# Moving GpSimd's sums of x1T ahead of other sums, and dealing the steps anew, in a graph kernel on one core

## The chip, the core and the metric

The kernel runs on one core of a Trainium2 chip. The metric is the device time of one execution in microseconds (us); of several runs the median is given.

## What is computed

The reference takes a batch of 64 graphs with 256 nodes and 512 features, x (64, 256, 512), a dense weighted adjacency adj (64, 256, 256), a node mask, and weights of 512 x 512, all float32:

```python
h = relu(adj @ (x @ W1) + b1)
h = relu(adj @ (h @ W2) + b2)
x1 = layernorm(x + adj @ (h @ W3) + b3)
q, k, v = x1 @ Wq, x1 @ Wk, x1 @ Wv
agg = adj @ (k * mask)
w = mask * sum(q * agg, axis=-1) / sqrt(512)
out = layernorm(x1 + softmax(w over the nodes) * v)
```

The layer norms have no weights. The kernel uses that q * agg summed over features is the row-wise product of x1 @ M with adj @ (mask x1), where M is the product of Wq and the transpose of Wk. So Wk is never applied to a batch.

## The kernel before

**Tiling.** Two graphs are a pair, so there are 32 pairs. A pair goes through three stages, each written as a Python generator that issues a few instructions at every step:

- `front` (F): the three layers of the first network. Per layer, `support` (L225) multiplies activations by W, and `aggregate` (L244) multiplies by adj and applies relu. The third layer ends with its support. 29 steps.
- `back` (B): adj times the third support (the steps "t"), plus x and b3; the first layer norm, which gives x1; adj @ (mask x1), called `gather` in the code (the steps "g"); and per graph the **double product** x1 @ [Wv | M] (`attention`, L422, the steps "A"), with the score w.
- `finish` (E): softmax of w over the nodes, its product with v, the sum with x1, the second layer norm, the output.

In round i, F works on pair i, B on pair i - 1 and E on pair i - 2. The strings `ORDER`, `START` and `END` (L507 to L509) say in which order the three are advanced, one letter for one step. `START` is for the first round, where B is `make_m` (L174), which computes M; `END` is for the last, where F is done. The instructions are thus laid out by hand[...].

**Seven products instead of eight.** Supports, adj products and the double product all go through `seven` (L96). It splits both operands into 2 x 2 blocks and computes the product with seven block products, P1 to P7, in the order P1, P7, P6, P2, P5, P3, P4, one per step. The price is sums: of the stationary operand, four tiles S (`a_sums`, L203, or `adj_sums` for adj), and of the moving one, four tiles T (`b_sums`, L84). P1, P6, P5 and P3 accumulate in one PSUM bank. After P1, P6 and P5 ScalarE copies the bank out (L103, L112, L120), and the next of them may write only then. P7 and P4 share a second bank; after P5, VectorE reads it for the fourth block, and P4 may write only then. In `seven` the only own product between P6 and P5 is P2, and between P5 and P3 there is none, so what stands there comes from the other stages.

A product of a support or of the double product is a *long* step on TensorE, one of an adj product (L285) a *short* one. An aggregate has four long steps, named by their output column blocks: c2, c3, c0, c1.

**Sums.** `a_sums` returns three functions: `first` issues S[2] (L211, needed by P7), `rest` issues S[0] and S[1] (L214 and L215, needed by P5 and P6), `last` issues S[3] (L218, needed by P3). For the activations hT, `first` is issued after c3, `rest` after c1, `last` inside the next support. For x1T, the transposed x1, all three are issued after the gather (L468 to L470), in a step of their own without a product. In the text they are S2, S0, S1 and S3. All of them run on GpSimd, the last round's sums of x1T excepted. GpSimd also makes the T sums of the adj products (L87 to L90), adds x to copies (L65), adds b3 to x (L65), and sums adj (L65).

**x1T.** Except in the last round, VectorE transposes 32 x 32 blocks of x1 (L407), SP writes them to DRAM (L410, "via") and reads them back as x1T in four transfers (L412). In the last round TensorE transposes (L398).

**Loads.** SP's queue issues all DMAs: xT, the four blocks of W1, adj, the biases, W2, W3, the second adj, b3 and the mask, in this order. A W block comes as 128 x 2 x 256, 256 KB. VectorE makes the T sums of W1, W2 and W3 as soon as they arrive, then `mask_s` (L166), and only then the first sums of the supports. adj of pair i + 2 is loaded right after the gather (L467).

**Buffers.** [...] There are 11 S tiles, 4 T tiles, 7 support tiles, one x1T and two adj tiles.

Of the kernel before, what the change touches and what calls it, by code (L numbers as in the profile page):

```python
# [9 lines left out]
FP = mybir.dt.float32  # L10
# [4 lines left out]
P = 128  # L15
PAIR = 2
G = PAIR
# [3 lines left out]
def gcn_then_graph_attention(ctx: ExitStack, tc: tile.TileContext, xT, xN, adjT, mask, W1, b1, W2, b2, W3, b3,  # L21
# [15 lines left out]
    nc = tc.nc  # L37
    NPAIR = xT.shape[0]
    N, D = 256, 512
    NH, DC = N // P, D // P  # L40
    HD = D // 2
# [4 lines left out]
    const = ctx.enter_context(tc.tile_pool(name="const", bufs=1))  # L46
# [5 lines left out]
    E = mybir.EngineType  # L52
    ctx.enter_context(tc.manual_schedule(engines={E.PE, E.DVE, E.Activation, E.Pool, E.SP}))

    def bank(shape=(P, G, N)):
        return psum.tile(list(shape), FP, name="ps", tag="ps")

    def tmp():
        return pool.tile([P, D], FP, name="tmp", bufs=6)
# [5 lines left out]
        nc.gpsimd.tensor_tensor(o, a, b, op=op)  # L65


    def load_xT(i):
        t = pool.tile([P, DC, G, N], FP, name="xT", bufs=1)
        nc.sync.dma_start(t, xT[i].rearrange("p (c g n) -> p c g n", c=DC, g=G))  # L70
        return [t[:, :2], t[:, 2:]]

    def load_adj(i):
        t = pool.tile([P, NH, G, N], FP, name="aT", bufs=2)
        nc.sync.dma_start(t, adjT[i].rearrange("p (k g n) -> p k g n", k=NH, g=G))
        return t
# [7 lines left out]
    def b_sums(B, Ts, eng):  # L84

        sub = OP.subtract
        eng.tensor_tensor(Ts[2], B[3], B[1], op=sub)  # L87
        eng.tensor_tensor(Ts[0], B[1], B[0], op=sub)  # L88
        eng.tensor_tensor(Ts[1], B[3], Ts[0], op=sub)  # L89
        eng.tensor_tensor(Ts[3], B[2], Ts[1], op=sub)  # L90
# [43 lines left out]
    def load_w(w, n):  # L134


        q = []
        for k in (1, 0):
            for j in range(2):
                if (k, j) == (1, 1):  # L140
                    t = tmp().rearrange("p (c f) -> p c f", c=2)
                else:
                    t = const.tile([P, 2, HD], FP, name=f"w{n}_{k}{j}")
                q.append(t)
                nc.sync.dma_start(t, w[k * HD:(k + 1) * HD, j * HD:(j + 1) * HD].rearrange("(c p) f -> p c f", p=P))
        ts = [const.tile([P, 2, HD], FP, name=f"w{n}_{s}") for s in KEYS]
        b_sums(q, ts, nc.vector)
        return {1: q[0], 2: q[2], 3: q[3], 4: ts[3], 5: ts[0], 6: ts[1], 7: ts[2]}

    xTs = load_xT(0)  # L150
    wl = [load_w(W1, 1)]
    aTs = {0: load_adj(0)}
    bcol = []
    for n, b in ((1, b1), (2, b2)):
        t = const.tile([P, DC], FP, name=f"b{n}")
        nc.sync.dma_start(t, b)
        bcol.append(t)
    wl.append(load_w(W2, 2))
    wl.append(load_w(W3, 3))
    aTs[1] = load_adj(1)  # L160
    b3b = const.tile([P, D], FP, name="b3b")
    nc.sync.dma_start(b3b, b3.partition_broadcast(P))
# [1 line left out]
    nc.sync.dma_start(mask_t, mask.rearrange("p (h b) -> p h b", h=NH))  # L164
    mask_s = const.tile([P, NH, NPAIR * G], FP, name="mask_s")
    nc.vector.tensor_scalar(mask_s, mask_t, ISCALE, None, op0=OP.mult)  # L166
    ident = const.tile([P, P], FP, name="ident")
    make_identity(nc, ident)
    eps = const.tile([P, 1], FP, name="eps")
    nc.vector.memset(eps, EPS)  # L170

# [2 lines left out]
    def make_m():  # L174

        wq = pool.tile([P, DC, D], FP, name="wqT", tag="r", bufs=1)
        qk = [[wq[:, d] for d in range(DC)],
              [pool.tile([P, D], FP, name="wkT", tag="T", bufs=4) for _ in range(DC)]]
        for d in range(DC):
            for t, w in ((qk[0][d], WqT), (qk[1][d], WkT)):  # L180
                nc.sync.dma_start(t, w[d * P:(d + 1) * P, :])
        m = [pool.tile([P, 2, D], FP, name="m0", tag="v", bufs=2), const.tile([P, 2, D], FP, name="m1")]
        v0 = const.tile([P, 2, D], FP, name="v0")
        nc.sync.dma_start(v0, Wv[:HD].rearrange("(c p) f -> p c f", p=P))
        v1 = const.tile([P, 2, D], FP, name="v1")
        nc.sync.dma_start(v1, Wv[HD:].rearrange("(c p) f -> p c f", p=P))
        yield
        for f in range(DC):
            pt = bank((P, D))
            for d in range(DC):  # L190
                for j in range(DC):
                    nc.tensor.matmul(pt[:, j * P:(j + 1) * P], lhsT=qk[0][d][:, f * P:(f + 1) * P],  # L192
                                     rhs=qk[1][d][:, j * P:(j + 1) * P], start=(d == 0 and j == 0),
                                     stop=(d == DC - 1), skip_group_check=True)
            nc.scalar.copy(m[f // 2][:, f % 2, :], pt)
            yield
        ts = [const.tile([P, 2, D], FP, name=f"mv_{s}") for s in KEYS]
        b_sums((v0, m[0], v1, m[1]), ts, nc.gpsimd)
        mv.update({1: v0, 2: v1, 3: m[1], 4: ts[3], 5: ts[0], 6: ts[1], 7: ts[2]})
        yield  # L200

# [72 lines left out]
    def t_sums(B):  # L274
        Ts = [pool.tile([P, G, HD], FP, name="T", tag="T", bufs=4) for _ in range(4)]
        b_sums((B[0][0], B[0][1], B[1][0], B[1][1]), Ts, nc.gpsimd)
        return Ts
# [76 lines left out]
    def back(i, C, aS, x, end):  # L354
# [20 lines left out]
        b = i * G  # L375
# [11 lines left out]
        hg = [(h, g) for h in range(NH) for g in range(G)]  # L387
        xmb = [[xm[:, :, h, j * HD:(j + 1) * HD] for j in range(2)] for h in range(2)]
        if end:
            x1T = pool.tile([P, 2, 2, G, N], FP, name="x1T", bufs=1)  # L390
            x1b = lambda h, k: x1T[:, k, :, :, h * P:(h + 1) * P]
            for h, g in hg:
                apply(h, g)
            Ts = t_sums(xmb)
            for h, g in hg:
                pt = bank((P, 2, 2, P))
                for c in range(DC):
                    nc.tensor.transpose(pt[:, c // 2, c % 2], r[:, g, h, c * P:(c + 1) * P], ident)  # L398
                (nc.scalar.copy if h else nc.vector.tensor_copy)(x1T[:, :, :, g, h * P:(h + 1) * P], pt)
        else:  # L400
            tr = pool.tile([P, 4, 32, NH, 2, 2, G], FP, name="tr", tag="gt", bufs=1)
            x1T = pool.tile([P, P, NH, 2, 2, G], FP, name="x1T", bufs=1)
            x1b = lambda h, k: x1T[:, :, h, k].rearrange("p n c g -> p c g n")
            for h, g in hg:
                apply(h, g)
                for k in range(2):
                    nc.vector.transpose(tr[:, :, :, h, k, :, g].rearrange("p q j c -> p c q j"),  # L407
                                        r[:, g, h, k * HD:(k + 1) * HD].rearrange("p (c q j) -> p c q j", c=2, q=4))
            via = dram.tile([4, P, D], FP, name="via")
            nc.sync.dma_start(via.rearrange("q p e -> p q e"), tr.rearrange("p q j h k c g -> p q (j h k c g)"))  # L410
            for q in range(4):
                nc.sync.dma_start(x1T[q * 32:(q + 1) * 32].rearrange("p (a j) h k c g -> p a (j h k c g)", a=4),  # L412
                                  via[q].rearrange("(a i) e -> i a e", a=4))
            yield
            Ts = t_sums(xmb)
# [3 lines left out]
        w = small.tile([P, NH, G], FP, name="w", bufs=2)  # L419
        vs = [None] * G  # L420

        def attention(g):  # L422
# [12 lines left out]
            def c22(ps, t):  # L435
# [5 lines left out]
        gather = adj_times(aS, xmb, Ts, lambda y, t: add(gb(0, 0), y, t), lambda x: nc.scalar.copy(gb(0, 1), x),  # L441
                           lambda v, t: add(gb(1, 0), v, t), lambda v, t: add(gb(1, 1), v, t))
        src, first, rest, last = a_sums(x1b, nc.vector if end else nc.gpsimd)
        if end:
            first()
            rest()
            last()
            one = attention(0)
            for k in "GMGMGMGMGGGMMM":
                next(gather if k == "G" else one)  # L450
                yield
            for _ in gather:
                pass
            for _ in one:
                pass
            tail = finish(i, (r, vs, w), [0])
            for _ in attention(1):
                next(tail, None)
                yield
            for _ in tail:  # L460
                pass
            for _ in finish(i, (r, vs, w), [1]):
                pass
            return
        yield from gather
        if i + 2 < NPAIR:
            aTs[i + 2] = load_adj(i + 2)  # L467
        first()  # L468
        rest()
        last()  # L470
        yield
        for g in range(G):
            yield from attention(g)
        return r, vs, w
# [29 lines left out]
            nc.sync.dma_start(out[i, :, g * NH * D:(g + 1) * NH * D].rearrange("p (h f) -> p h f", h=NH), vs[g])  # L504


    ORDER = ("F E F" + " B F" + " B F E" * 5 + " B F B F F B B F F B F" + " B F"*3 + " B F E"*3 + " B E F E" + " B F E B B F B B F B F B" + " B F B B F B B F B F B")  # L507
    START = "F" * 12 + "F B" * 6
    END = "E B B B E" + "B" * 5 + "B E" * 10  # L509

    def run(order, **gens):
# [11 lines left out]
    xS, first, rest, last = a_sums(lower_first(xTs))  # L523
# [3 lines left out]
    for i in range(NPAIR + 1):  # L527
# [8 lines left out]
        if prev is not None:  # L536
            gens["E"] = finish(i - 2, prev)
        order = START if i == 0 else ORDER if i < NPAIR else END
        res = run(order.replace(" ", ""), **gens)
        if i > 0:  # L540
            prev = res["B"]
        if i < NPAIR:
            C, aS, x, xTs, xS = res["F"]
# [36 lines left out]
```

## Time and profile before

| what | value |
|---|---|
| median of three runs | 2885.65 us (2885.42 to 2885.7) |
| span of the profiled execution | 2883.9 us |
| granted clock of TensorE, mean | 0.997 |
| TensorE's first matmul | 6.78 us |
| busy: VectorE, ScalarE, GpSimd | 1130.0, 938.8, 1426.2 us |
| GpSimd, S<-x1T: L211, L214, L215, L218 | 2.19, 1.99, 1.52, 1.51 us each |
| GpSimd, S<-hT: the same lines | 1.27, 1.27, 1.30, 1.27 us each |
| ScalarE, copy of a bank (L103, L112, L120) | 0.58 us |
| DMA queue of SP | 189.10 MB, 20.4% of 16 engines |

PE in the profile is TensorE, PEld its weight loads, DVE VectorE, ACT ScalarE, POOL GpSimd, SP the queue of DMAs. A row of the timeline merges equal instructions that follow each other: start, time, engine, line, operation, output <- inputs, count, and in brackets the idle time ahead and what ended it. A matmul of float32 counts as two records, so a long step is x8 with 256 columns or x4 with 512, and a short step x4 with 256. Matmuls overlap, and their ends are modelled, so the distance between starts tells more than the duration. `ps<-mv_T,S` of L428 is P7, P6 or P5 of the double product, `ps<-m,S` its P3, `ps<-w,S` of L232 a support's P3.

### The profile page before, as it was taken

Reading aid. Unit: us, or ns where it says so; the run is one execution under the profiler, and the core shown is the slowest. Engines: PE = TensorE matmul, PEld = TensorE weight load, DVE = VectorE, ACT = ScalarE, POOL = GpSimd, SP = SyncE. Lnnn points to the kernel's source line nnn. Section 1 sums busy time; section 2 is a strip of 40 time slices with the busy share of each in tenths; the row PEclk is TensorE's granted clock in tenths of the full one; section 3 lists DMA queues with packets and bytes.
Section 4 is the critical chain, followed back from the end, with each engine's and each line's share of the span. In section 5 each row is a group of like instructions: output and inputs, shape, how many; then the busy total and the mean of one; then the engine's idle time right before and its main releaser. Section 6 shows DMA issues by size and latency. Waiting matters only on the chain.

```text
span 2883.9 us, 29739 instructions
## 1 busy us (share of the span) xinstructions
PE 2821.4 (98%) x11284; PEld 2174.5 (75%) x11284; DVE 1130.0 (39%) x2322; ACT 938.8 (33%) x1517; POOL 1426.2 (49%) x1126
## 2 busy tenths in 40 slices
PE   8999999999999999999999999999999999999996
PEld 7787777777777777777777777777787777777773
DVE  1344234443344433344433444333444334443345
ACT  2333233332333332333223333323332233333233
POOL 3635455354554454553545544555535455445542
PEclk9999999999999999999999999999999999999998
DMA  4211222211222112222022221122221222211210
GB/s 151 66 51 44 66 81 81 81 36 60 66 81 80 48 48 66 81 81 74 37 66 66 81 81 44 52 66 81 81 66 43 64 70 81 81 44 51 66 59 30
DMA packets 62942, 191.00 MB, mean 66 GB/s; under 512 B 5712, under 2 KB 8912, under 8 KB 54608
## 3 DMA queue, kind: packets, MB, share of 16 engines
q1 hardware_dynamic: 62800, 189.10, 20.4%
q8 instruction: 90, 1.47, 0.2%
q14 instruction: 52, 0.43, 0.0%
HBM read 123.02 MB, written 66.06 MB: 66 GB/s over the span
## 4 chain that ended last, share of the span: by engine, by line
PE 62%; POOL 18%; issue 17%; ACT 1%; DVE 1%; DMA 0%; POOLq 0%; ACTq 0%; SPq 0%; DVEq 0%
PE ps L232 27%; PE ps L428 23%; PE ps L285 7%; PE ps L253 4%; POOL S L211 4%; POOL S L214 4%; POOL S L215 3%; POOL T L88 2%; POOL T L89 1%; POOL T L87 1%; POOL T L90 1%; POOL S L218 1%; ACT hT L256 1%; PE ps L192 0%; PE ps L319 0%
## 5 line engine op out<-in xcount | busy, mean ns | idle before, releaser
L232 PE MATMUL ps<-w_T,S 128*128 128x256 f32 x2304 | 548.2, 381 | 1.7 <-POOL S L211 1.1
L232 PEld LDWEIGHTS ps<-w_T,S 128*128 128x128 f32 x2304 | 433.9, 191 | 106.2 <-issue 51.4
L253 PE MATMUL ps<-aT,sup 128*128 128x256 f32 x2048 | 467.7, 379 | 0.0
L253 PEld LDWEIGHTS ps<-aT,sup 128*128 128x128 f32 x2048 | 389.6, 190 | 62.5 <-issue 7.4
L62 DVE TENSOR_TENSOR sup<-ps,tmp 128x512 f32<-128x512 f32 x288 | 198.8, 691 | 582.5 <-PE ps L232 337.4
L428 PE MATMUL ps<-mv_T,S 128*128 128x512 f32 x768 | 359.2, 597 | 29.1 <-POOL S L215 29.1
L112 ACT COPY tmp<-ps 128x512 f32<-128x512 f32 x224 | 131.1, 585 | 684.4 <-PE ps L428 269.1
L211 POOL TENSOR_TENSOR S<-hT 128x512 f32<-128x512 f32 x64 | 81.4, 1272 | 536.0 <-ACT hT L256 536.0
L65 POOL TENSOR_TENSOR tmp<-tmp,x 128x512 f32<-128x512 f32 x96 | 120.4, 1269 | 432.1 <-ACT tmp L120 293.3
L62 DVE TENSOR_TENSOR v<-ps,tmp 128x512 f32<-128x512 f32 x128 | 88.6, 692 | 577.1 <-PE ps L428 573.8
L428 PEld LDWEIGHTS ps<-mv_T,S 128*128 128x128 f32 x768 | 143.4, 190 | 188.5 <-issue 121.9
L256 ACT ACTIVATE hT<-ps,b 128x512 f32<-128x512 f32 x256 | 174.8, 683 | 302.9 <-PE ps L253 302.9
L103 ACT COPY tmp<-ps 128x512 f32<-128x512 f32 x224 | 130.5, 583 | 361.4 <-PE ps L232 237.3
L232 PE MATMUL ps<-w,hT 128*128 128x256 f32 x1024 | 241.9, 379 | 0.0
L428 PE MATMUL ps<-v,x1T 128*128 128x512 f32 x512 | 240.7, 593 | 0.0
L120 ACT COPY tmp<-ps 128x512 f32<-128x512 f32 x224 | 131.1, 585 | 317.8 <-PE ps L428 186.0
L232 PEld LDWEIGHTS ps<-w,hT 128*128 128x128 f32 x1024 | 194.7, 190 | 49.5 <-issue 22.2
L285 PE MATMUL ps<-T,aS 128*128 128x256 f32 x768 | 200.4, 383 | 0.3 <-ACT tmp L103 0.3
L87 POOL TENSOR_TENSOR T<-sup 128x512 f32<-128x512 f32 x32 | 40.4, 1264 | 309.3 <-ACT sup L234 309.3
L232 PE MATMUL ps<-w,S 128*128 128x256 f32 x768 | 186.4, 386 | 1.5 <-ACT tmp L120 0.8
L428 PEld LDWEIGHTS ps<-v,x1T 128*128 128x128 f32 x512 | 141.8, 291 | 46.9 <-issue 2.9
L232 PEld LDWEIGHTS ps<-w,S 128*128 128x128 f32 x768 | 140.8, 190 | 46.9 <-issue 25.6
(107 smaller groups left out, 4085.3 us busy)
## 6 DMA issues: line engine op xcount, KB each, us to landing
xT<-in_xT SPq DMA_DIRECT2D x32, 1024.0 KB, 4.9
x<-in_xN SPq DMA_DIRECT2D x32, 1024.0 KB, 5.8
out<-v SPq DMA_DIRECT2D x64, 512.0 KB, 2.8
via<-tr SPq DMA_DIRECT2D x31, 1024.0 KB, 4.3
x1T<-via SPq DMA_DIRECT2D x124, 256.0 KB, 4.7
aT<-in_adjT SPq DMA_DIRECT2D x32, 512.0 KB, 3.5
w<-in_W SPq DMA_DIRECT2D x9, 256.0 KB, 5.4
wqT<-in_WqT SPq DMA_DIRECT2D x4, 256.0 KB, 5.8
```

Of the source, the lines that this page charges most:

```text
L62: nc.vector.tensor_tensor(o, a, b, op=OP.add)
L65: nc.gpsimd.tensor_tensor(o, a, b, op=op)
L103: nc.scalar.copy(t1, x)
L112: nc.scalar.copy(u, x)
L120: nc.scalar.copy(q, x)
L211: eng.tensor_tensor(S[2], blk(0, 0), blk(1, 0), op=sub)
L214: eng.tensor_tensor(S[0], blk(1, 0), blk(1, 1), op=OP.add)
L232: nc.tensor.matmul(ps[:, g], lhsT=src[n][:, c, g], rhs=w[n][:, c], start=(first and g == 0 and c == 0), stop=(g == G - 1 and c == 1), skip ...
L253: nc.tensor.matmul(ps[:, g], lhsT=C[k][c // 2][:, g, (c % 2) * P:(c % 2 + 1) * P], rhs=aT[:, k, g], start=(g == 0 and k == 0), stop=(g == ...
L256: nc.scalar.activation(hT[c // 2][:, c % 2], ps, AF.Relu, bias=b[:, c:c + 1])
L285: nc.tensor.matmul(ps[:, g], lhsT=aS[n][:, g], rhs=mov[n][:, g], start=(first and g == 0), stop=(g == G - 1), skip_group_check=True)
L428: nc.tensor.matmul(ps, lhsT=src[n][:, c, g], rhs=mv[n][:, c], start=(first and c == 0), stop=(c == 1), skip_group_check=True)
```

## The change

1. In `back`, the three functions of x1T's sums are issued after the fourth step of the gather instead of after its seventh. The step without a product is gone. adj of pair i + 2 is still loaded after the gather.
2. `ORDER` and `START` are written anew. In the supports of the first two layers two short steps stand between P5 and P3 where there was one. Around the second aggregate, P1 of the double product now stands ahead of the aggregate's c0, P7 between c0 and c1, P6 behind c1. In the first round the four steps of `make_m` that have products stand at other places: behind P5 of the second support, ahead of P1, behind P7 and behind P5 of the third.
3. The T sums of [Wv | M], four of 128 x 1024, go from GpSimd to VectorE, in the first round.
4. The first load of xT is split: its second half, then the bottom left, top right and bottom right blocks of W1, then the first half of xT, then the top left block. The blocks of W2 and W3 come in that order too; before it was bottom left, bottom right, top left, top right.
5. The identity is made at the start, and ten matmuls of identity with identity, into a bank that nobody reads, stand ahead of everything else on TensorE. Twenty more stand in the last round behind P4 of the step "t", ahead of the transposes of x1.

The core of the diff:

```diff
-    def load_xT(i):
+    def load_xT(i, between=None):
         t = pool.tile([P, DC, G, N], FP, name="xT", bufs=1)
-        nc.sync.dma_start(t, xT[i].rearrange("p (c g n) -> p c g n", c=DC, g=G))
+        src = xT[i].rearrange("p (c g n) -> p c g n", c=DC, g=G)
+        if between is None:
+            nc.sync.dma_start(t, src)
+        else:
+            nc.sync.dma_start(t[:, 2:], src[:, 2:])
+            between()
+            nc.sync.dma_start(t[:, :2], src[:, :2])
...
+        def begin():
+            for b in (0, 3, 1):
+                load(b)
+
+        def end():
+            load(2)
+            b_sums(q, ts, nc.vector)
...
+    def warm(n):
+
+        ps = bank((P, P))
+        for _ in range(n):
+            nc.tensor.matmul(ps, lhsT=ident, rhs=ident, start=True, stop=True)
+
+    warm(10)
+    begin, end = load_w(W1, 1)
+    xTs = load_xT(0, begin)
+    wl = [end()]
...
-        b_sums((v0, m[0], v1, m[1]), ts, nc.gpsimd)
+        b_sums((v0, m[0], v1, m[1]), ts, nc.vector)
...
         if end:
+            warm(20)
...
+        for _ in range(4):
+            next(gather)
+            yield
+        first()
+        rest()
+        last()
         yield from gather
         if i + 2 < NPAIR:
             aTs[i + 2] = load_adj(i + 2)
-        first()
-        rest()
-        last()
-        yield
         for g in range(G):
             yield from attention(g)
...
-    ORDER = ("F E F" + " B F" + " B F E" * 5 + " B F B F F B B F F B F" + " B F"*3 + " B F E"*3 + " B E F E" + " B F E B B F B B F B F B" + " B F B B F B B F B F B")
-    START = "F" * 12 + "F B" * 6
+    ORDER = ("F E F" + " B F" + " B F E" * 2 + " B B E F E F" + " B F E" + " B F B F F B B F F" +
+             " B F B F B F E B B E F F" + " B F E B F E" + " B F E B F E B B F B F B F B" + " B F B F B B F B F B F B")
+    START = "F" * 4 + "B" + "F" * 12 + "B" + "F" * 6 + "B FF B FFF B F B F"
```

More of the change, by code (lines that the diff above doesn't have):

```diff
@@ L134, in load_w, with load @@
     def load_w(w, n):
[L137 to L145, printed above, removed]
-        ts = [const.tile([P, 2, HD], FP, name=f"w{n}_{s}") for s in KEYS]
[L147 to L151, printed above, removed]
+        q = [tmp().rearrange("p (c f) -> p c f", c=2) if b == 1 else
+             const.tile([P, 2, HD], FP, name=f"w{n}_{b}") for b in range(4)]
+        ts = [const.tile([P, 2, HD], FP, name=f"w{n}_{s}") for s in KEYS]
+        def load(b):
+            k, j = 1 - b // 2, b % 2
+            nc.sync.dma_start(q[b], w[k * HD:(k + 1) * HD, j * HD:(j + 1) * HD].rearrange("(c p) f -> p c f", p=P))
+        def begin():
[4 more added lines that the diff above has]
+            b_sums(q, ts, nc.vector)
+            return {1: q[0], 2: q[2], 3: q[3], 4: ts[3], 5: ts[0], 6: ts[1], 7: ts[2]}
+        return begin, end
+    ident = const.tile([P, P], FP, name="ident")
+    make_identity(nc, ident)
+    def warm(n):
[6 more added lines that the diff above has]
+    wl = [end()]
     aTs = {0: load_adj(0)}
@@ L157, in gcn_then_graph_attention @@
         bcol.append(t)
-    wl.append(load_w(W2, 2))
-    wl.append(load_w(W3, 3))
+    for n, w in ((2, W2), (3, W3)):
+        begin, end = load_w(w, n)
+        begin()
+        wl.append(end())
     aTs[1] = load_adj(1)
@@ L166, in gcn_then_graph_attention @@
     nc.vector.tensor_scalar(mask_s, mask_t, ISCALE, None, op0=OP.mult)
-    ident = const.tile([P, P], FP, name="ident")
-    make_identity(nc, ident)
     eps = const.tile([P, 1], FP, name="eps")
```

## The prediction

> **What bounds the kernel now.** I read three views: the page for the engine that sets the end, the waits of that engine for what it loses, and its timeline for one period, to put a place to each loss.
>
> From the page and from the view of TensorE's waits (who waits for whom: us in total, times, longest):
>
> ```profile
> PE 2821.4 (98%) x11284; PEld 2174.5 (75%) x11284; DVE 1130.0 (39%) x2322; ACT 938.8 (33%) x1517; POOL 1426.2 (49%) x1126
> PE ps L428 <- POOL S L215: 29.1, 31, 1.0
> PE ps L232 <- DMA w<-in_W: 6.8, 1, 6.8
> PE ps L398 <- DVE r L385: 5.5, 2, 5.1
> ```
>
> TensorE is the bound, and one wait, once in each of 31 periods, is half of its idle time (2883.9 - 2821.4 = 62.5 us). Busy is not peak, so I go by the distance between starts. One period of TensorE's timeline (start us, us, engine and line, tiles, count):
>
> ```profile
> 1062.36 1.97 PE L232 MATMUL ps<-w,S 128*128 128x256 f32 x8
> 1064.17 1.03 PE L285 MATMUL ps<-T,aS 128*128 128x256 f32 x4
> ...
> 1086.69 1.03 PE L285 MATMUL ps<-xm,aT 128*128 128x256 f32 x4
> 1087.62 1.97 PE L232 MATMUL ps<-w,S 128*128 128x256 f32 x8
> 1089.42 1.03 PE L285 MATMUL ps<-T,aS 128*128 128x256 f32 x4
> ...
> 1098.92 1.88 PE L428 MATMUL ps<-v,x1T 128*128 128x512 f32 x4
> 1100.64 1.89 PE L253 MATMUL ps<-aT,sup 128*128 128x256 f32 x8
> 1102.36 1.88 PE L428 MATMUL ps<-mv_T,S 128*128 128x512 f32 x4
> 1105.19 1.99 PE L428 MATMUL ps<-mv_T,S 128*128 128x512 f32 x4 [0.95 <-POOL S L215]
> 1107.01 1.89 PE L232 MATMUL ps<-w,hT 128*128 128x256 f32 x8
> ```
>
> An undisturbed long step takes 1.72 to 1.73 us from start to start (1098.92 to 1100.64), a short one, of L285, 0.86. Against that, P7 and P6 of the double product take 4.65 (1102.36 to 1107.01) where 3.44 would do: **1.21 us lost**. P3 of the first support takes 1.81, 0.08 over; the short step ahead of P3 of the second support 0.93 and P3 itself 1.80, 0.07 + 0.07 over. Sum 1.43 us in a period of 88.34 us (the softmax transposes of L304 start at 1051.37 and 1139.71). Two smaller losses, by the transposes of L319 (0.24) and P6 of the second support (0.08), are not touched.
>
> GpSimd's timeline of the same period shows why P6 waits:
>
> ```profile
> 1084.63 1.27 POOL L218 TENSOR_TENSOR S<-hT,S 128x512 f32<-128x512 f32 x1
> 1098.16 1.27 POOL L211 TENSOR_TENSOR S<-hT 128x512 f32<-128x512 f32 x1 [12.26 <-ACT hT L256]
> 1099.39 2.19 POOL L211 TENSOR_TENSOR S<-x1T 128x512 f32<-128x512 f32 x1
> 1101.56 1.99 POOL L214 TENSOR_TENSOR S<-x1T 128x512 f32<-128x512 f32 x1
> 1103.62 1.52 POOL L215 TENSOR_TENSOR S<-S,x1T 128x512 f32<-128x512 f32 x1
> ```
>
> The sums of x1T could have run earlier: the last of the four x1T transfers is issued at 1088.94 and the slowest lands 5.3 us after its issue, at 1094.3. They stand behind S<-hT, which waits for ScalarE's hT until 1098.16, so S1 (L215) is done only at 1105.14. GpSimd sits idle for 12.26 us meanwhile.
>
> In the first pair, TensorE's timeline shows what else is lost:
>
> ```profile
> 66.40 1.99 PE L232 MATMUL ps<-w_T,S 128*128 128x256 f32 x8 [1.12 <-POOL S L211]
> 68.96 1.99 PE L232 MATMUL ps<-w_T,S 128*128 128x256 f32 x8 [0.57 <-POOL S L215]
> 75.17 1.97 PE L232 MATMUL ps<-w,S 128*128 128x256 f32 x8 [0.77 <-ACT tmp L120]
> ```
>
> [...] landed x1T, idle GpSimd, and its sums 5.1 us later (1094.3 to 1099.39). [...] Here S<-x1T of L211 takes 2.19 us on GpSimd and 1.20 on VectorE, in the last pair. [...] Here matmuls follow each other at 427 ns from 6.78 us on, and at 216 from 12.7.
>
> **The change part by part.**
>
> *Sums of x1T ahead of the other sums.* Nothing is added; GpSimd's four instructions now stand after L218 and ahead of S<-hT. They wait for x1T, and S<-hT, then the sums of the third support, aS, x + b3 and the sums of xT are queued behind. From landing at 1094.3, S1 is done 5.75 later (1099.39 to 1105.14 today), at 1100.05; S3 after 7.35, at 1101.65. P6 of the double product, without its wait, starts at 1102.36 + 1.72 - 0.22 (the three P3 losses, gone) = 1103.86: **3.8 us of slack**. P1, which reads x1T itself, moves one long step forward (c0 now follows it): 1098.92 - 1.73 - 0.22 = 1096.97, 2.7 us after the landing. S<-hT ends at 1102.9 and is wanted by the third support's P7; between P6 and it stand P6, P2, P5 and one support step, so that is 1103.86 + 6.89 = 1110.75. S1 of that support: c1 ends at 1103.86, ScalarE takes 0.9, L214 and L215 2.6: 1107.4, wanted at 1110.75 + 3.45 = 1114.2. The aS, b3 and xT sums come some microseconds earlier than today. The load of adj stays behind the gather; outputs go out one step apart around it, and x is loaded about a microsecond later, wanted by GpSimd only after aS. Gain: 31 x 1.21 = **37.5 us**.
>
> *Steps dealt anew.* Between P5 and P3 of both per-period supports stand two short steps, 1.73 us, instead of one of 0.86. What ScalarE needs from the end of P5 is 0.86 + 0.08 = 0.94 (or 0.86 + 0.14 = 1.00 in the second). So all of it is hidden: 31 x 0.22 = **6.8 us**. I went through every place of the new order where a product overwrites a bank that ScalarE or VectorE must first read: the smallest distance is 1.73 us, so no new place of this kind arises. VectorE's normalization steps move by one or two places; scores are done 1.1 us after P3 and read at 3.4.
>
> *The products of Wq and Wk dealt anew, their sums on VectorE.* The first pair's four groups, 3.6 us each, now stand at P5/P3 of two supports, ahead of P1 of the third, and behind its P7. Its P6 then comes 3.6 + 3.45 + 3.6 us after the last hT step, against 3.5 needed. The three waits above vanish: their steps take 3.02 (63.38 to 66.40), 2.56, 1.83, 2.65 (72.52 to 75.17) and 1.80, against 1.73 each: **3.2 us**. VectorE gets four sums of 128x1024, at twice the 0.69 us of a 128x512 row 5.5 us, late in the first pair; behind them stands C10, which TensorE wants some 10 us later: cost 0.
>
> *First loads in parts, W in another order.* The bytes are the same, and the loads arrive back to back, 256 KB in 0.75 us. TensorE can start near 5.5 instead of 6.78, but the end of the first support hangs on VectorE: P4 (21.18) may overwrite its bank after the add that ends at 20.69, and this is behind the sums of all three W and mask_s (19.26). W3's first sum needs its third block now and not its fourth, so it starts 0.75 earlier; mask_t lands at 18.64, so mask_s moves to about 18.7 and P4 to 20.2. Gain **0.9 us**, from 0 (P3 late, by the clock or the second half of xT) to 1.5.
>
> *Idle matmuls.* Ten at the start: 20 records of 0.22 us at half clock end near 5.9, before VectorE lets anything count: 0. Twenty in the last pair, 40 records of 0.11 us, 4.5 us at full clock, lie in the idle 5.07 us ahead of the transposes of L398 (2826.4 to 2831.46): hidden. At half clock they would take 9 and push the transposes by up to 3.5. What full clock saves there is mostly behind VectorE's own queue. I take 0, from -1 to +3.5.
>
> Sum: 37.5 + 6.8 + 3.2 + 0.9 = 48.4. The profiled span of 2883.9 becomes 2835.5; unprofiled runs read 1.75 above the span (2885.65 to 2883.9), so **2837.2 us**.
>
> **The rivals.**
>
> *The wait moves to another place.* Something in the new order that I place with slack, such as x1T's landing for P1 (2.7 us), is late. Against it: over all periods x1T lands at most 6.2 us after issue, 0.9 later than here. If 0.4 us of the 1.43 comes back: 2837 + 12 = 2849.
>
> *Slower: GpSimd and TensorE both held by x1T.* The sums now wait for a DMA at the head of GpSimd's queue, and P1 reads x1T a step earlier. Each microsecond of landing beyond 1096.97 costs 31 us; the gain (48.4 / 31 = 1.56 a period) is used up if x1T lands 4.3 us later. At 4.8 us later: 31 x 2.1 = 65, or 2902. For it: write and re-read of x1T are two dependent transfers. Against it: nothing is moved ahead of them on SP's queue, and the DMA engines are 20% busy.
>
> *It doesn't do what it says.* If GpSimd's order hardly moved, 6.8 + 3.2 + 0.9 = 10.9 would be left: 2875. Against it: the new order of instructions has them ahead of S<-hT.
>
> **How the numbers follow.** Forecast 0.82, moved wait 0.11, GpSimd's order unmoved 0.03, slower 0.04. This kernel can be told from no change at about 0.2%, 5.8 us. The first three are faster: 0.95 after rounding down, 0.04 slower, 0.01 within. The range takes the bounds of start and tail and part of the moved wait: 2833 to 2846.
>
> **What would show it.** A period of 86.9 us between the softmax transposes; no wait of P6 for S1; GpSimd's S<-x1T ahead of S<-hT, starting before P1 of the double product; P3 of the supports at 1.73; 62.5 us of idle TensorE near 20. I am wrong if P1 or P6 of the double product waits for x1T or its sums, or if a short step shows a new wait in each period.

## The result and the profile after

| | before | after |
|---|---|---|
| median of four runs | 2885.53 us (2885.28 to 2885.7) | **2839.06 us** (2837.91 to 2840.06) |
| ratio | | 0.9839 (95% interval 0.9822 to 0.9856) |
| span of the profiled execution | 2883.9 us | 2836.1 us |
| its own time | 2885.65 us | 2837.91 us |
| TensorE idle in it | 62.5 us | 26.1 us |

The change makes the kernel 1.6% faster. The forecast was 2837.2 us.

First the page of the changed kernel: the busy line, the engines of the chain that ended last, and the group of the double product's sums, whose last number is the idle time just ahead of it:

```profile
PE 2810.0 (99%) x11344; PEld 2191.4 (77%) x11344; DVE 1120.9 (40%) x2326; ACT 945.3 (33%) x1517; POOL 1437.5 (51%) x1122
...
PE 97%; DVE 1%; DMA 1%; ACT 1%; issue 0%; SPq 0%; POOL 0%; ACTq 0%; DVEq 0%; POOLq 0%
...
L451 PE MATMUL ps<-mv_T,S 128*128 128x512 f32 x768 | 361.0, 592 | 0.0
```

In the chain before, other engines than TensorE still had a large part:

```profile
PE 62%; POOL 18%; issue 17%; ACT 1%; DVE 1%; DMA 0%; POOLq 0%; ACTq 0%; SPq 0%; DVEq 0%
```

Now TensorE alone has 97%. The line of the double product (L428 before, L451 now) waits for nothing on its sums. TensorE's waits now begin so (total, times, longest):

```profile
PE ps L341 <- DVE e L334: 3.7, 2, 2.5
PE ps L421 <- DVE r L407: 2.2, 2, 1.1
PE ps L307 <- ACT tmp L126: 1.6, 2, 1.0
PE ps L254 <- POOL S L237: 1.5, 1, 1.5
```

The number of times is the one to read: nothing happens 31 times any more. All of these waits lie in the first or the last round. The first row of before, 29.1 us in 31 waits, has no successor.

TensorE's timeline of one period, with the short steps between P5 and P3 of a support first, and then the double product:

```profile
1067.35 1.03 PE L307 MATMUL ps<-xm,aT 128*128 128x256 f32 x4
1068.22 1.03 PE L307 MATMUL ps<-T,aS 128*128 128x256 f32 x4
1069.08 1.89 PE L254 MATMUL ps<-w,S 128*128 128x256 f32 x8
1070.81 1.89 PE L254 MATMUL ps<-w_T,hT 128*128 128x256 f32 x8
...
1077.71 1.88 PE L451 MATMUL ps<-v,x1T 128*128 128x512 f32 x4
1079.43 1.89 PE L275 MATMUL ps<-aT,sup 128*128 128x256 f32 x8
1081.16 1.88 PE L451 MATMUL ps<-mv_T,S 128*128 128x512 f32 x4
1082.87 1.89 PE L275 MATMUL ps<-aT,sup 128*128 128x256 f32 x8
1084.60 1.88 PE L451 MATMUL ps<-mv_T,S 128*128 128x512 f32 x4
1086.32 1.88 PE L451 MATMUL ps<-v,x1T 128*128 128x512 f32 x4
```

The starts are 0.87, 0.86, 1.73 apart in the support and 1.72 or 1.73 throughout the double product: no step is longer than an undisturbed one. GpSimd's timeline of the same period tells why:

```profile
1065.29 1.27 POOL L240 TENSOR_TENSOR S<-hT,S 128x512 f32<-128x512 f32 x1
1075.06 2.19 POOL L233 TENSOR_TENSOR S<-x1T 128x512 f32<-128x512 f32 x1 [8.49 <-DMA x1T<-via]
1077.20 2.01 POOL L236 TENSOR_TENSOR S<-x1T 128x512 f32<-128x512 f32 x1
1079.29 1.52 POOL L237 TENSOR_TENSOR S<-S,x1T 128x512 f32<-128x512 f32 x1
1080.89 1.52 POOL L240 TENSOR_TENSOR S<-x1T,S 128x512 f32<-128x512 f32 x1
1082.37 1.27 POOL L233 TENSOR_TENSOR S<-hT 128x512 f32<-128x512 f32 x1
```

The first sum of x1T is released by the transfer itself, 0.12 us after its landing (1074.94), and S<-hT follows the four. S1 (L237) is done at 1080.81, 3.8 us ahead of P6 at 1084.60. P1 reads x1T at 1077.71, 2.8 us after the landing. The landing varies, though: over the 31 periods of this profile P1 starts 1.1 to 2.9 us after it.

**Where the 47.83 us went from** (starts of the softmax transposes in both timelines as markers):

| stretch | before | after | gain |
|---|---|---|---|
| start to the first transposes | 168.13 | 163.11 | 5.02 |
| 29 periods, mean of one | 88.33 | 86.90 | 41.35 |
| the period after them | 86.59 | 85.17 | 1.42 |
| the last round | 67.73 | 67.69 | 0.04 |

### The profile page after: what moved, and what is told of

Its sections match the earlier page's. It is cut to its first block, busy times and chain, and to the rows that moved or that the text cites. A ratio compares the mean times of both kernels' runs of the same rounds, so it can differ in the third digit from the quotient of the medians.

```text
span 2836.1 us, 29920 instructions
## 1 busy us (share of the span) xinstructions
PE 2810.0 (99%) x11344; PEld 2191.4 (77%) x11344; DVE 1120.9 (40%) x2326; ACT 945.3 (33%) x1517; POOL 1437.5 (51%) x1122
## 3 DMA queue, kind: packets, MB, share of 16 engines
q8 instruction: 90, 1.47, 0.2%
## 4 chain that ended last, share of the span: by engine, by line
PE 97%; DVE 1%; DMA 1%; ACT 1%; issue 0%; SPq 0%; POOL 0%; ACTq 0%; DVEq 0%; POOLq 0%
PE ps L254 41%; PE ps L451 27%; PE ps L275 16%; PE ps L307 13%; PE ps L214 1%; DMA aT<-in_adjT 0%; PE ps L341 0%; PE ps L326 0%; DMA mask_t<-in_mask 0%; ACT v L526 0%; SPq L149 0%; DVE st L517 0%; POOL tmp L65 0%; DMA out<-v 0%; DVE st L388 0%
## 5 line engine op out<-in xcount | busy, mean ns | idle before, releaser
L451 PE MATMUL ps<-mv_T,S 128*128 128x512 f32 x768 | 361.0, 592 | 0.0
L451 PE MATMUL ps<-v,x1T 128*128 128x512 f32 x512 | 240.6, 592 | 0.0
L451 PEld LDWEIGHTS ps<-mv_T,S 128*128 128x128 f32 x768 | 145.8, 190 | 102.1 <-issue 92.3
L233 POOL TENSOR_TENSOR S<-x1T 128x512 f32<-128x512 f32 x31 | 67.9, 2190 | 275.7 <-DMA x1T<-via 275.7
L307 PE MATMUL ps<-T,aS 128*128 128x256 f32 x768 | 200.3, 383 | 0.3 <-ACT tmp L109 0.3
L451 PEld LDWEIGHTS ps<-v,x1T 128*128 128x128 f32 x512 | 146.2, 290 | 69.3 <-issue 17.7
L233 POOL TENSOR_TENSOR S<-hT 128x512 f32<-128x512 f32 x64 | 81.2, 1269 | 220.5 <-ACT hT L278 220.5
```

The costliest lines, as they stand in the source:

```text
L233: eng.tensor_tensor(S[2], blk(0, 0), blk(1, 0), op=sub)
L307: nc.tensor.matmul(ps[:, g], lhsT=aS[n][:, g], rhs=mov[n][:, g], start=(first and g == 0), stop=(g == G - 1), skip_group_check=True)
L451: nc.tensor.matmul(ps, lhsT=src[n][:, c, g], rhs=mv[n][:, c], start=(first and c == 0), stop=(c == 1), skip_group_check=True)
```

## The experiments

**Sums of x1T late again.** In the changed kernel the three calls go back behind the gather; all else stays:

```diff
-        for _ in range(4):
-            next(gather)
-            yield
-        first()
-        rest()
-        last()
         yield from gather
         if i + 2 < NPAIR:
             aTs[i + 2] = load_adj(i + 2)
+        first()
+        rest()
+        last()
```

> The kernel after with the sums of x1T issued behind the whole gather again; all else as after. Theory (the place of the sums on GpSimd's queue is the gain): they stand behind S<-hT again, S1 is done 1.06 us after P6 of the double product could start, the wait of some 1.0 us with its slow first matmul is back in each of 31 periods: period 88.1 us instead of 86.9, in all 2839 + 37.5 = 2876 us. Rival (the new order of steps, with c1 between P7 and P6, hides the wait by itself): period 86.9, 2839 us.

Measured: 2876.46 us in one run, 37.4 above the changed kernel. The period is 88.085 us, 1.185 more, or 36.7 in 31 periods; 1.7 us more come from the last round, of which below. Between the two profiled spans it is 38.5. TensorE's waits of this kernel:

```profile
PE ps L451 <- POOL S L233: 25.3, 31, 0.8
```

The wait is back 31 times. It is P7 that stands here, for the first sum (L233, which starts at 1093.03 in GpSimd's timeline, behind S<-hT), and no longer P6: with the steps dealt anew P7 comes earlier against the sums. The timeline around it:

```profile
1092.56 1.89 PE L275 MATMUL ps<-aT,sup 128*128 128x256 f32 x8
1095.26 1.99 PE L451 MATMUL ps<-mv_T,S 128*128 128x512 f32 x4 [0.82 <-POOL S L233]
1097.09 1.89 PE L275 MATMUL ps<-aT,sup 128*128 128x256 f32 x8
1098.81 1.98 PE L451 MATMUL ps<-mv_T,S 128*128 128x512 f32 x4
1100.62 1.88 PE L451 MATMUL ps<-v,x1T 128*128 128x512 f32 x4
```

The idle time is 0.82 a time and the loss of period 1.185. From the start of the step ahead to P7 it takes 2.70 us, 0.97 over the pace of 1.73; P7 takes 1.83 to the next start, 0.11 over, and the next step of the double product 1.81. So its idle time alone understates this wait.

**Only the sums early.** The kernel before, with the three calls behind four steps of the gather, everything else as it was (a step without a product is kept, so that the letters of the order mean the same):

```diff
-        yield from gather
-        if i + 2 < NPAIR:
-            aTs[i + 2] = load_adj(i + 2)
+        for _ in range(4):
+            next(gather)
+            yield
         first()
         rest()
         last()
         yield
+        yield from gather
+        if i + 2 < NPAIR:
+            aTs[i + 2] = load_adj(i + 2)
```

> The kernel before with only the sums of x1T issued behind the gather's fourth step; order of steps, loads and first round as before. Theory: no wait of P6 for S1, the three losses at P3 stay: period 88.33 - 1.21 = 87.12 us, in all 2885.5 - 37.5 = 2848 us. Rival (early sums need the new order, because GpSimd then waits for x1T ahead of S<-hT and holds something else): a new wait of TensorE in each period, 2855 us or more.

Measured: 2848.43 us, one run. The period is 87.126 us against 88.33: 1.20 us, 37 us in 31 periods. The steps dealt anew are what is left of the way to 86.90: 0.226 a period, 7.0 in all. None of TensorE's waits for GpSimd in this profile comes more than once. The two parts of the period are told apart, from both sides.

**Only the start.** The kernel before, with the new `START` and the sums of M and Wv on VectorE:

```diff
-        b_sums((v0, m[0], v1, m[1]), ts, nc.gpsimd)
+        b_sums((v0, m[0], v1, m[1]), ts, nc.vector)
...
-    START = "F" * 12 + "F B" * 6
+    START = "F" * 4 + "B" + "F" * 12 + "B" + "F" * 6 + "B FF B FFF B F B F"
```

> The kernel before with the first round alone changed: the new START and the T sums of [Wv | M] on VectorE. Theory: the three waits of the third support at 66.4, 69.0 and 75.2 us vanish and nothing else moves: 3.2 us less before the first softmax transposes (168.13 to 164.9 us), in all 2882.3 us. Rival (VectorE's 5.5 us of sums, ahead of C10, hold a product of the second round): under 2 us are gained, and a wait of L285 for sup or T shows near 75 us.

Measured: 2882.45 us, one run. The first transposes start 3.69 us earlier; 0.47 of it is already there at the first aggregate (22.44 against 22.91 us, ahead of every product that this edit moves; TensorE's clock was full from 11.16 us on in this run and from 12.72 in the one of before, so I put it down to the run), which leaves 3.22. The period is 88.331, unchanged.

**x1T landed late.** The forecast rested on 2.7 us of slack between the landing of x1T and P1, and priced what would happen without it. Here x1 is written to DRAM twice, which puts the read back by one write:

```diff
-            nc.sync.dma_start(via.rearrange("q p e -> p q e"), tr.rearrange("p q j h k c g -> p q (j h k c g)"))
+            for _ in range(2):
+                nc.sync.dma_start(via.rearrange("q p e -> p q e"), tr.rearrange("p q j h k c g -> p q (j h k c g)"))
```

> The kernel after with x1 written to DRAM twice before x1T is read back, so that x1T lands later; the result is the same. Theory (P1 of the double product has 2.7 us of slack on x1T's landing, its sums 3.8): landing some 3 to 4.3 us later, each period is longer by the delay less 2.7 us, 0.3 to 1.6 us, in all 2849 to 2889 us; the wait is at P1 of L451 for x1T, not at its sums. Rival (the slack is smaller, GpSimd held at the head of its queue passes the delay on to the supports): longer by the whole delay, 2930 us or more.

Measured: 2932.43 us, one run, above what the theory gave and in the region of the rival. In the period that corresponds to the timelines above, it takes 15.45 us from the issue of the first write to the last landing, where the changed kernel takes 10.97: x1T is 4.48 us late, 1.7 more than the slack (over all periods the medians are 15.5 and 11.2). TensorE's waits (the matmuls of P1 have line 452 here):

```profile
PE ps L452 <- DMA x1T<-via: 57.0, 28, 3.0
PE ps L452 <- issue: 5.2, 3, 1.9
```

All 31 waits are P1's for x1T itself (three have no releaser in the profile, but they too end 0.2 us after the landing); P6 and P7 wait for no sum. That is the place that the theory named, and most periods are 88.7 to 89.2, some 2.1 longer. In the period just used it is 2.04: 1.71 beyond the slack, 0.14 from landing to start, and the rest in slower steps behind the wait. But twelve periods are 90.3 to 92.6. In two of these x1T landed later still, and P1 waited 2.6 and 2.9 us. In the ten others something else came on top. TensorE's timeline of one:

```profile
302.34 3.62 PE L452 MATMUL ps<-v,x1T 128*128 128x512 f32 x4 [2.09 <-DMA x1T<-via]
305.75 2.07 PE L275 MATMUL ps<-aT,sup 128*128 128x256 f32 x8
307.66 1.88 PE L452 MATMUL ps<-mv_T,S 128*128 128x512 f32 x4
```

P1 takes 3.41 us to the next start instead of 1.72, with no further wait. The view by windows gives the clock (stretch, its length, busy time of PE, PEld, DVE, ACT and POOL each with a count, granted clock, DMA share, GB/s):

```profile
295.86:299.27 3.41, 3.41 (x18) 3.00 (x17) 1.88 (x3) 1.98 (x3) 0.00 (x0) 1.00 1.00 211
299.27:302.69 3.42, 1.33 (x6) 0.90 (x5) 0.00 (x0) 1.39 (x2) 0.38 (x1) 1.00 1.05 286
302.69:306.10 3.41, 3.41 (x5) 1.45 (x5) 0.00 (x0) 0.05 (x1) 3.41 (x2) 0.50 0.29 119
306.10:309.51 3.41, 3.41 (x13) 2.23 (x12) 0.00 (x0) 1.92 (x3) 3.25 (x4) 1.00 0.00 0
```

In the second window TensorE was busy for 1.33 of 3.42 us; in the third the granted clock is 0.50; then it is full again (1.00). Ten such windows at half clock, each worth 1.7 us by the 3.41 less 1.72 of this P1, are an estimated 17 us; the mean clock of this run is 0.993, where the changed kernel has 0.998. The waits are 62 us, and further waits of L307 2.7. What is left is much the same in every period, with or without a fall of the clock: 0.34 us beyond the idle time (88.94 is 86.90 + 1.70 of idle + 0.34), about as in the kernel with the sums late (1.185 - 0.82 = 0.37). In 31 periods these are 11 us, and some 92 of the 94 us of longer span are accounted for.

**No idle matmuls.** One kernel without the ten at the start (`warm(10)` removed), one without the twenty at the end (`warm(20)` removed).

> The kernel after without the ten idle matmuls at the start. Theory (the end of the first support hangs on VectorE's queue, not on the clock): P1 and P7 run at half clock, P4 starts at 20.7 us as in the kernel after, 2839 us, same within 1 us. Rival (the clock counts): the first support ends 1 to 3 us later, 2840 to 2842 us.

> The kernel after without the twenty idle matmuls of the last round. Theory (runs of the kernel after lie 2.2 us apart, those of before 0.4[...]): runs within 0.5 us of each other, median 2838 to 2839.5 us, so nothing is lost without them. Rival (they save the time of the transposes at half clock): 0.5 to 2 us slower. Second rival (the spread comes from the start): it stays at 2 us.

Measured: 2839.54 us (2838.22 to 2840.95) without the first, 2838.97 (2838.69 to 2839.94) without the second; ratios to before 0.9841 (0.9827 to 0.9854) and 0.9839 (0.9826 to 0.9853), where the changed kernel has 0.9839. Neither can be told from nothing. Without the ten, the clock is full from 10.9 us on instead of 4.6, and yet the first aggregate starts at 22.64 against 22.54: the P4 ahead of it waits for VectorE's add in both (0.84 us without the ten, 0.77 with them). Without the twenty, the clock is half for 6.83 us ahead of the transposes of the last round, and the round still takes 42.34 us to the next softmax transposes, as with them (42.35). The theory that these twenty make the runs spread fails: without them the runs still lie 1.25 us apart, and not within 0.5.

**Loads whole.** The changed kernel with the first xT in one transfer and the W blocks in the old order:

```diff
-            for b in (0, 3, 1):
+            for b in (0, 1, 2):
...
-            load(2)
+            load(3)
...
-    xTs = load_xT(0, begin)
+    xTs = load_xT(0)
+    begin()
```

> The kernel after with the first load of xT undivided and the W blocks in the order of before. Theory (the end of the first support hangs on VectorE behind all loads, which are the same bytes): the first support ends up to 0.4 us later than in the kernel after, 2839.0 to 2839.5 us. Rival (the early start of P1 counts): 1 to 2 us slower, 2840 to 2841 us.

Measured: 2838.36 us (2838.15 to 2840.05), ratio 0.9838 (0.9824 to 0.9851). The first support ends 0.34 later, as its theory allowed, and the first transposes start at 163.44, 0.33 later, which is less than this start differs between two profiles of the same loads (163.11 here, 163.67 without the last idle matmuls). The loads' part is worth nothing that can be told.

**W3's sums late.** In the changed kernel VectorE still makes W3's sums and `mask_s` ahead of the first support's adds. Here these are issued behind that support:

```diff
+    late = []
...
-        wl.append(end())
+        wl.append(end(n == 2))
...
-    nc.vector.tensor_scalar(mask_s, mask_t, ISCALE, None, op0=OP.mult)
+    late.append(lambda: nc.vector.tensor_scalar(mask_s, mask_t, ISCALE, None, op0=OP.mult))
...
         C = yield from support(src, wl[0])
+        while late:
+            late.pop(0)()
```

(`end(False)` puts its `b_sums` into the same list.)

> The kernel after with VectorE's T sums of W3 and mask_s issued behind the first support of the first pair instead of ahead of its sums. Theory (P4 of the first support waits for VectorE, whose queue stands behind W3 and the mask): P4 starts right behind P3, near 19.7 instead of 20.7 us, 1.0 us less, 2838 us. Rival (something else, such as adj or the copies, holds the aggregate behind it): under 0.3 us.

Measured: 2839.18 us (2836.96 to 2839.46), ratio 0.9836 (0.9823 to 0.985): no gain in the median. In the profile the start did gain: aggregate at 22.00, first transposes 0.55 earlier. That is half of the 1.0 us expected: P4 does follow P3 at once, at 20.27, but P3 itself starts at 18.47 instead of 17.98. The last round lost 1.70, 44.05 us instead of 42.35. The view by windows of this kernel in the last round:

```profile
2795.34:2798.75 3.41, 3.02 (x11) 1.55 (x9) 0.71 (x2) 3.41 (x7) 0.00 (x0) 1.00 0.16 64
2798.75:2802.16 3.41, 1.67 (x7) 1.20 (x8) 1.29 (x2) 1.11 (x3) 0.00 (x0) 1.00 0.62 244
2802.16:2805.57 3.41, 3.41 (x7) 1.61 (x5) 0.69 (x1) 0.00 (x0) 0.00 (x0) 0.50 0.00 0
```

The same pattern as above: a window of 3.41 us with 1.67 busy, then one at half clock. The idle time is made of two waits, P3 and P4 of the gather; in the changed kernel's own timeline they are these:

```profile
2797.71 1.03 PE L307 MATMUL ps<-T,aS 128*128 128x256 f32 x4
2799.70 1.13 PE L307 MATMUL ps<-xm,aS 128*128 128x256 f32 x4 [0.97 <-ACT tmp L126]
2801.99 1.10 PE L307 MATMUL ps<-T,aT 128*128 128x256 f32 x4 [1.16 <-DVE gt L62]
2802.93 1.88 PE L451 MATMUL ps<-mv_T,S 128*128 128x512 f32 x4
```

The order of this round has P5, P3 and P4 of the gather in a row. In the changed kernel's profile they fell into two windows (0.97 us of idle from 2796.72 to 2800.13, 1.16 in the next), and the clock was 1.00 in both and in the one behind. So the same code took 42.35 us in the profile with the two waits in two windows, and 44.05 in the one with 1.74 us of idle in a single window. The other profiles agree: the kernel with the sums late again, whose last round is the same code, took 44.06 us there, with both waits in one window (2.13 us idle) and half clock after it; x1T late, no idle matmuls at the start and loads whole took 42.34 or 42.35.

**Two steps of the last round exchanged.** If that is so, taking away one of the two waits must remove the loss, and the spread of runs as far as it comes from there. P2 of the double product is put between P5 and P3 of the gather:

```diff
-            for k in "GMGMGMGMGGGMMM":
+            for k in "GMGMGMGGMGGMMM":
```

One kernel has this alone, one together with W3's sums late.

> The changed kernel with two neighbouring steps of its last round exchanged: P5 of the gather is issued ahead of P2 of the double product, so that P2 stands between P5 and P3. In the changed kernel P3 and P4 of the gather wait 0.97 and 1.16 us there, 2.3 us apart, and in another run of it these two waits were followed by 3.41 us of half clock (1.7 us). Theory (the two waits are what drops the clock at the end, in some runs): P3 can start when ScalarE's copy, one activation earlier than before, is done, some 0.7 us earlier, P4 follows VectorE's add some 2 us earlier than now, and less than 1.5 us of idle are left in this place; the last round from the transposes of the softmax to the next ones goes from 42.35 to 40.3 us, the clock stays full to the end, time 2837.0, and the runs lie within 1 us of each other. Rival 1 (the spread of 2 us has another cause, such as the landing of the first loads): 2837.0, but the runs still spread by 2 us. Rival 2 (VectorE's wait for the output buffer of v sets this place, not the order): round unchanged at 42.3, time 2839.

> The same exchange in the last round, in the kernel in which the T sums of W3 and mask_s are issued behind the first support of the first pair (which started the first transposes 0.55 us earlier, but lost 1.70 us in its last round to 3.41 us of half clock). Theory: both gains stand, 0.55 at the start and 2.0 at the end, no half clock: 2836.5, some 0.5 us below the other kernel of this call, runs within 1 us. Rival (the half clock at the end comes from something else): 2837 to 2839 with a spread of 2 us.

Measured: 2836.19 us (2836.07 to 2836.72, five runs), ratio 0.9829 (0.9816 to 0.9842), and 2835.34 us (2835.02 to 2837.24, four runs), ratio 0.9827 (0.9813 to 0.984). The first kernel's timeline:

```profile
2796.29 1.03 PE L307 MATMUL ps<-T,aS 128*128 128x256 f32 x4
2797.15 1.88 PE L451 MATMUL ps<-v,x1T 128*128 128x512 f32 x4
2799.28 1.13 PE L307 MATMUL ps<-xm,aS 128*128 128x256 f32 x4 [0.25 <-ACT tmp L126]
2800.25 1.03 PE L307 MATMUL ps<-T,aT 128*128 128x256 f32 x4
2801.11 1.88 PE L451 MATMUL ps<-mv_T,S 128*128 128x512 f32 x4
```

2.13 us of waits have become 0.25, the round takes 40.24 us, and the runs lie within 0.65 us where the changed kernel's lie within 2.15. Both rivals of this first kernel fail, with a caution: these two kernels ran on another chip than the changed one. The kernel before had the same median there (2885.52 us), but one of its nine runs took 2887.35, so a single run can be 2 us late without this pair of waits.

The second kernel is faster by 0.85 in the median, of which the earlier start gave 0.6. But one of its four runs, 2837.24, is 1.6 us or more above the others, so its theory, runs within 1 us, fails, and what delayed that run is open. The profile is of another run (2835.66): it has one half-clock window, at 2776.82, behind one with 1.8 us of idle. This fell on the idle matmuls and the step ahead of them, and the round still took 40.36 us. This kernel is the fastest of all here, 3.7 us below the changed one.

## Why the prediction was right

| term of the sum | forecast | measured |
|---|---|---|
| sums of x1T early | 37.5 | 37.2 (period 88.326 to 87.126, alone) |
| steps dealt anew | 6.8 | 7.0 (87.126 to 86.90) |
| products and sums of M, Wv | 3.2 | 3.22 (alone) |
| first loads | 0.9 | 0.37 in these two profiles, nothing that can be told over all |
| idle matmuls | 0 | 0 |
| sum, of spans | 48.4 | 47.83 |

**The main step, the order on GpSimd, is shown.** Taken back, it costs 36.7 to 37.4 us; made alone, it gives 37. GpSimd's order came out as forecast, and so did the two slacks in the period that the forecast worked with: 2.8 us for P1 (forecast 2.7) and 3.8 for P6. Over all periods P1's is as small as 1.1, so there was less room than the forecast's 2.7. The late x1T shows that the first is real and is the one that decides: delayed by 1.7 us more than it, P1 waits. In the traces GpSimd sat idle for 12.26 us before, up to the S<-hT that stood first in its order, and made the sums of x1T only behind it, 5.1 us after the landing; now it is 0.12 us from landing to sum.

**Steps dealt anew and the start** come out to 0.2 us, as what the other parts leave, and to 0.02 us, by the start alone; that the second is so close is luck, as this start differs by some tenths from profile to profile. P3 of the supports follows at 1.73 as forecast, and no short step waits in the period. So the rival of a wait that moves to another place has nothing to show. One of the signs is off: TensorE is idle for 26.1 us and not near 20.

**First loads: the term that was mis-sized.** The step put W3's first sum 0.75 us earlier and `mask_s` to about 18.7, on a landing of mask_t at 18.64, which was read from the kernel before. Two lines of the changed kernel's timeline show what came instead:

```profile
18.33 0.69 DVE L96 TENSOR_TENSOR w_T<-w,w_T 128x512 f32<-128x512 f32 x1
19.22 0.23 DVE L190 TENSOR_SCALAR mask_s<-mask_t 128x128 f32<-128x128 f32 x1 [0.20 <-DMA mask_t<-in_mask]
```

W3's sums begin at 16.28 instead of 16.60, 0.32 earlier, but mask_t lands at 19.20, 0.56 later, and `mask_s` waits for it. So `mask_s` moves by 0.04. That P4 still moves by 0.47 (21.18 to 20.71) has another reason, which P3 and P4 before and after show:

```profile
19.38 1.97 PE L232 MATMUL ps<-w,S 128*128 128x256 f32 x8 [0.72 <-issue]
21.18 1.89 PE L232 MATMUL ps<-w_T,xT 128*128 128x256 f32 x8
...
17.98 1.96 PE L254 MATMUL ps<-w,S 128*128 128x256 f32 x8 [0.72 <-issue]
20.71 1.99 PE L254 MATMUL ps<-w_T,xT 128*128 128x256 f32 x8 [0.77 <-DVE sup L62]
```

The step took P4 to be held by VectorE's add in both kernels. Before, in this profile, it was not: the add ended at 20.69, and P4 came 0.49 later, right behind P3, so TensorE itself was late. After, TensorE is early, and P4 waits for the add, which ends at 20.66, hardly sooner. In two other profiles of the old start, where the clock is full from 10.96 and 11.16 us on and not only from 12.72, P4 is held by VectorE as the step has it and starts at 20.90 and 20.61. So I put most of the 0.37 us down to the later full clock in the profile of before (12.72 us), and to luck. Over all profiles nothing can be told: in the three with the old start of the code mask_t lands at 18.64 to 18.84 and the first aggregate starts at 22.44 to 22.91; in the six with the loads divided, W3's sums early and `mask_s` ahead of the adds, it is 19.20 to 19.82 and 22.54 to 23.16. The later landing takes away what W3's earlier sums could give. Why it is later is open: with the first xT undivided it was still 19.54.

**Idle matmuls at nothing** are confirmed at both ends, as far as the profiles show: P4 at the start and the last transposes wait for VectorE with them and without. The ten take 4.03 us from 1.36 on and end at 5.39, where the forecast had 5.9.

**The 1.9 us by which the median lies above the forecast** are 0.6 from the sum of spans, and 1.15 from the median of the runs standing above the profiled run (2839.06 to 2837.91). The forecast took 1.75 from span to run, with the 0.4 us spread of before. The changed kernel's runs spread by 2.15, and the exchange of two steps, which removes a pair of waits in the last round, brings this to 0.65, on another chip; with the sums of W3 late as well it is 2.22 again. That the runs above 2839 had the half-clock window is inferred and not shown: of their clock only the mean is on record, 0.998 as in the profiled run, and one such window would move it by an estimated 0.0006 (half of 3.41 us in 2836).

**The slower rival had the right mechanism and too low a price.** It put each microsecond beyond the slack at 31 us. The measured kernel, 1.7 us beyond by landing, lost 94 and not 53. The waits themselves took 62, as 2.0 a period, since x1T lands later still in some; what a wait costs beyond its idle time took 11, and the clock 17, and the price had left out both. At 4.5 us later the rival's price would give 2892 us, where 2932 was measured. The point from which the gain is used up is thus probably nearer than the rival's 4.3 us; no run stands there.

## What to carry to other kernels

Where an engine sits idle behind one wait while other inputs have landed (GpSimd for 12.26 us here), reorder its instructions by when inputs arrive and when results are wanted; check the slack of both, for the operand itself as well as for the sums. Price a wait on TensorE by the distance between starts (0.82 us of idle came with 1.185 us of longer period here), and ask what else lies idle close to it: two waits of 0.97 and 1.16 us, their ends 2.3 us apart, were followed by 3.41 us at half clock in one profile (a round of 44.05 us) and by none in another (42.35). A kernel whose runs spread more after a change than before (2.15 us against 0.4 here) can have something in it that depends on chance; look for it in the clock record of single profiles.

## What was not expected of the hardware

**Half clock behind idle time.** In the profiles before and after, the granted clock stood for 2812.58, 10.24, 40.96 and 2822.82 us between two of its changes, which is 824, 3, 12 and 827 times 3.413 us; the windows here have this length and begin where the clock changes. Their place against the first instruction differs between runs (the first change to full clock is at 4.61 us in the changed kernel and at 5.13 with the loads whole). Half clock came behind a window with 2.09 us of idle in the kernel with the late x1T, behind one with 1.74, made of two waits, in the kernel with W3's sums late, and behind one with 1.76 in the kernel before (2821.89 to 2825.30; there it lasted 10.24 us, of which the first two windows had 2.32 and 2.74 us of idle). In the profiles before and after, every window at full clock with 1.47 us of idle or less was followed by full clock. In the period shown of the kernel with the late x1T the half clock lasts one window (302.69 to 306.10), in which TensorE is busy throughout, and P1 takes 1.7 us longer. What rule the clock follows is not shown by these runs.

**These waits cost more than their idle time.** The step that waited 0.82 us for a sum started 0.97 us behind its predecessor's pace and lost 0.11 itself; each period was 0.37 us longer than the idle time says. With x1T late it was 0.34.
